# A four-layer graph network: where x is loaded and split, and where layer 2 makes its first adjacency tiles

## The chip, the cores and the metric

The kernel runs on one core of one Trainium2 chip. The metric is device time in microseconds (us) from launch to end; less is better. Three runs of the kernel before gave 3312.99, 3316.28 and 3319.8 us, median 3316.28 us.

The engines are named as in the profile: PE (TensorE, matrix products), DVE (VectorE), ACT (ScalarE), POOL (GpSimd), SP (SyncE, which here only issues transfers). Each engine works through its own list of instructions in order. A transfer is issued from the list of SP, ACT or POOL, and so it waits behind whatever stands ahead of it there.

## The reference, cut to what matters

There are 4096 nodes with 256 features, and one 0/1 adjacency matrix of 4096 x 4096. Four layers follow each other, each `x = layernorm(x + layer(x, adj))`:

```python
# layer 0
deg = jnp.sum(adj, axis=1, keepdims=True)
agg = adj @ x / jnp.maximum(deg, 1.0)
relu(jnp.concatenate([x, agg], axis=-1) @ W + b)
# layer 1: two steps of  R @ Xf  and of a top-p attention  A @ Xa, with two weights each
# layer 2
neighbor_node_features = adj @ node_features
neighbor_edge_features = jnp.einsum('ij,ji->i', adj, edge_features)[:, None]
jnp.concatenate((node_features, neighbor_node_features, neighbor_edge_features), axis=1) @ weight + bias
# layer 3: relu(D^-1/2 (adj + I) D^-1/2 x W + b)
```

## The kernel before, in words

The rows are taken in 32 tiles of 128. A product of the adjacency with a feature matrix is, for one row tile, 32 matmuls of 128x128 by 128x512 that add up in one PSUM bank. The 512 columns are the 256 features twice: the upper bits of each number and the rest. `split` (L142) makes these two halves with three instructions. DVE masks the upper bits into a buffer `up` (L145), ACT copies them into the left half (L146), and DVE subtracts them from the source into the right half (L147).

`load_halves` (L149) does this for a whole feature matrix, in eight pieces of four row tiles, here called piece 0 to piece 7. A piece is 512 KB. It is loaded into one of two buffers of `scratch`, `up` has two more, and so the load of piece c+2 waits for the subtraction of piece c. The helper is called for x in layer 0 (L222, loads issued by ACT), for features inside layer 1, and for the product z of layer 2 (L1076, loads issued by SP).

Layer 0 has two buffers for its accumulators, named acc and nef, and the row tiles take them in turns. POOL loads the adjacency as half a row tile into `a8` (L250: from float32 in DRAM to bytes, five buffers), SP stores these bytes into `adj8_d` for the later layers (L251), and ACT converts a quarter of a row tile at a time from bytes into `a` (L253, four buffers, so one row tile). A buffer of `a` becomes free when PE has multiplied with it and DVE has added it into `sums` (L260, L262; L265 folds the sums). From the sums, PE makes the degrees (L272), DVE the reciprocal (L275 to L279), ACT and DVE the scaled neighbours `agg` (L284, L285); PE transposes `x0i` and `agg` (L180) and multiplies them with w0 (L294). Row tile 2 needs the accumulator of row tile 0, so it waits for the `agg` of row tile 0. In the lists of the engines, the row tiles overlap: the order comes from a scheduler that works on the program as it is written, and it can be read from the compiled program.

At the start `list_d`, two small tables in DRAM for layer 1, is filled from the tile `blank` (L124, on SP).

Layer 2 (L1075 on) reads z from `zu_d`, into which layer 1 writes its last rows by an indirect transfer of POOL (L763). `main` (L1087) loads a quarter row tile of bytes (L1091), converts it on ACT (L1093) and multiplies (L1096). `l2_end` (L1099) loads `x2i` and `u` (L1104, L1106), and DVE adds them (L1107, L1108). All these loads are on SP.

Of the kernel before, what the change touches and what calls it, by code (L numbers as in the profile page):

```python
# [11 lines left out]
F32 = mybir.dt.float32  # L12
I32 = mybir.dt.int32
U8 = mybir.dt.uint8
F32R = mybir.dt.float32r
# [6 lines left out]
P = 128  # L22
D = 256
# [25 lines left out]
def gnn_stack(ctx, tc, x, adjt, adjn, w0, b0, w1, w2t, w3t, u1t, u2t, ln_g, ln_b, w2, b2, w3, b3, out):  # L49
# [3 lines left out]
    nc = tc.nc  # L53
    N = x.shape[0]
    NT = N // P
    LC = min(512, N)
    NLC = N // LC
    JP = min(8, NT)
    NJP = NT // JP
    J0 = min(4, NT)  # L60
# [21 lines left out]
    def load_bcast(pool, src, name):  # L82
        t = pool.tile([P, src.shape[0]], F32, name=name)
        nc.scalar.dma_start(t, src[None, :].to_broadcast([P, src.shape[0]]))
        return t
# [26 lines left out]
    list_d = [dram.tile([N + P, 1], I32, name=f"list{n}_d") for n in range(STEPS)]  # L112

    adj8_d = [dram.tile([P, NT, P], U8, name=f"adj8_{it}_d") for it in range(NT)]
# [4 lines left out]
    blank = const.tile([P, NT], I32, name="blank")  # L119
    nc.gpsimd.iota(blank, pattern=[[1, NT]], base=0, channel_multiplier=NT)  # L120
    nc.vector.tensor_scalar(blank, blank, P - 1, None, op0=ALU.bitwise_and)
    nc.vector.tensor_scalar(blank, blank, float(N), None, op0=ALU.add)
    for t in list_d:
        nc.sync.dma_start(t[:N, :].rearrange("(p k) o -> p (k o)", k=NT), blank)  # L124

    def rows(t, it):
        return t[it * P : (it + 1) * P, :]

    def all_rows(t):
        return t.rearrange("(t p) d -> p t d", p=P)  # L130

    def load_w(pool, src, name):
        t = pool.tile([P, src.shape[0] // P, src.shape[1]], F32, name=name)
        nc.scalar.dma_start(t, src.rearrange("(c p) o -> p c o", p=P))
        return t
# [3 lines left out]
        nc.gpsimd.dma_start(t, src[it, :, c * jp : (c + 1) * jp, :])  # L139
        return t  # L140

    def split(up, dst, src):  # L142


        nc.vector.tensor_scalar(up, src.bitcast(I32), UPPER, None, op0=ALU.bitwise_and)  # L145
        nc.scalar.copy(dst[:, :, :D], up.bitcast(F32))  # L146
        nc.vector.tensor_sub(dst[:, :, D:], src, up.bitcast(F32))  # L147

    def load_halves(scratch, src, queue, cols=slice(None)):  # L149


        xh = hpool.tile([P, NT, 2 * D], F32R, tag="H", name="xh")
        W = J0 * D
        for c in range(NT // J0):
            s = slice(c * J0, (c + 1) * J0)
            t, up = (scratch[:, k * W : (k + 1) * W].rearrange("p (j d) -> p j d", d=D) for k in (c % 2, 2 + c % 2))
            if queue is None:
                t = src[:, s, :]
            else:
                queue.dma_start(t, all_rows(src)[:, s, cols])  # L160
            split(up.bitcast(I32), xh[:, s, :], t)
        return xh

    def adj_matmul(pool, acc, it, halves, piece, each=None):

        for c in range(NJP):
            a = piece(it, c)
            for j in range(JP):
                jt = c * JP + j
                nc.tensor.matmul(acc, a[:, j, :], halves(jt), start=(jt == 0), stop=(jt == NT - 1))  # L170
            if each is not None:
                each(c, a)
# [24 lines left out]
    def ln_apply(dst, t, stats):  # L197
        mv, r = stats
        nc.vector.tensor_scalar(dst, t, mv[:, 0:1], r, op0=ALU.subtract, op1=ALU.mult)
# [17 lines left out]
    with tc.tile_pool(name="l0", bufs=1) as l0, tc.tile_pool(name="l0w", bufs=2) as l0w:  # L217
# [1 line left out]
        nc.scalar.dma_start(w1_sb, w1)  # L219
        w2t_sb = l0.tile([DA, DA], F32, name="w2t_sb")  # L220
        nc.scalar.dma_start(w2t_sb, w2t)
        x0h = load_halves(l0.tile([P, 4 * J0 * D], F32, name="scratch"), x, nc.scalar)  # L222
        w0_sb = load_w(l0, w0, "w0_sb")
        lb_sb = load_bcast(l0, ln_b, "lb_sb")
        b0_sb = load_bcast(l0, b0, "b0_sb")
# [5 lines left out]
                nc.scalar.copy(wq_sb[:, c, h * DA : (h + 1) * DA], ps[:, :DA])  # L231
        for h in range(2):
            nc.scalar.dma_start(w3t_sb[:, :, h * DA : (h + 1) * DA], w3t.rearrange("(c p) o -> p c o", p=P))
        x1 = xpool.tile([P, NT, D], F32, tag="X", name="x1")
        deg1 = l0.tile([P, NT], F32, name="deg1")

# [74 lines left out]
        acc = None  # L311
        for it in range(NT + 1):
            if it >= 1:
                agg = l0_agg(acc, l0_degrees(it - 1, sums))
            if it < NT:
                acc, sums = l0_main(it)
# [9 lines left out]
    with tc.tile_pool(name="l1", bufs=1, reuse_waits="tile") as l1:  # L326
# [716 lines left out]
        for n in range(STEPS):  # L1043
            cur["n"] = n
            with tc.tile_pool(name=f"step{n}", bufs=2, reuse_waits="tile") as cur["w"], \
# [6 lines left out]
                else:  # L1052
# [3 lines left out]
                    for c in range(NLC):  # L1056
                        s = slice(c * GP, (c + 1) * GP)
# [4 lines left out]
                        k = kS[:, c * LC : (c + 1) * LC].rearrange("p (j d) -> p j d", d=P)  # L1062
# [3 lines left out]
                    for c in range(NJP):  # L1066
                        s = slice(c * JP, (c + 1) * JP)
# [5 lines left out]


    with tc.tile_pool(name="l23", bufs=1, reuse_waits="tile") as l23:  # L1075
        zh = load_halves(l23.tile([P, 4 * J0 * D], F32, name="scratch"), zu_d[:N, :], nc.sync, slice(0, D))  # L1076
        w2e_sb = load_bcast(l23, w2[2 * D, :], "w2e_sb")
        b2_sb = load_bcast(l23, b2, "b2_sb")
        w3_sb = load_w(l23, w3, "w3_sb")
        b3_sb = load_bcast(l23, b3, "b3_sb")  # L1080

        yh = [pool.tile([P, NT // 2, 2 * D], F32R, tag="X", name=f"yh{k}") for k, pool in enumerate((xpool, l23))]

        def y_halves(jt):
            return yh[2 * jt // NT][:, jt % (NT // 2), :]

        def main(it, halves):  # L1087
            acc = ps_acc.tile([P, 512], F32, tag=("acc", "nef")[it % 2], name="acc")
            for c in range(NJP):
                a8 = l23.tile([P, JP, P], U8, tag="a8", name="a8", bufs=5)  # L1090
                nc.sync.dma_start(a8, adj8_d[it][:, c * JP : (c + 1) * JP, :])  # L1091
                a = l23.tile([P, JP, P], F32R, tag="adjt", name="a", bufs=4)
                nc.scalar.copy(a, a8)  # L1093
                for j in range(JP):
                    jt = c * JP + j
                    nc.tensor.matmul(acc, a[:, j, :], halves(jt), start=(jt == 0), stop=(jt == NT - 1))  # L1096
            return acc

        def l2_end(it, acc):  # L1099
            nn = l23.tile([P, D], F32, tag="agg", name="agg", bufs=2)  # L1100
            nc.scalar.copy(nn, acc[:, :D])
            nc.vector.tensor_add(nn, nn, acc[:, D:])
            xi = l23.tile([P, D], F32, tag="res", name="x2i", bufs=2)
            nc.sync.dma_start(xi, rows(x2_d, it))  # L1104
            u = l23.tile([P, D], F32, tag="u", name="u", bufs=2)
            nc.sync.dma_start(u, rows(zu_d, it)[:, D:])  # L1106
            nc.vector.tensor_add(xi, xi, b2_sb)  # L1107
            nc.vector.tensor_add(u, u, xi)  # L1108
            t = l23.tile([P, D], F32, tag="t", name="t", bufs=2)
            nc.vector.scalar_tensor_tensor(t, w2e_sb, nef[:, it : it + 1], nn, op0=ALU.mult, op1=ALU.add)  # L1110
            nc.vector.tensor_add(t, t, u)
            x3 = l23.tile([P, D], F32, tag="h", name="x3", bufs=3)
            ln_apply(x3, t, ln_stats(t))
            nc.sync.dma_start(rows(x3_d, it), x3)
            return x3

        def l2_y(it, x3):
            xt = transposed(x3)
            ps = half("mm")
            for c in range(2):  # L1120
                nc.tensor.matmul(ps, xt[:, c, :], w3_sb[:, c, :], start=(c == 0), stop=(c == 1))  # L1121
            y = l23.tile([P, 1, D], F32, tag="y", name="y", bufs=2)
            nc.scalar.activation(y[:, 0, :], ps, AF.Copy, scale=dinv[:, it : it + 1])
            up = l23.tile([P, 1, D], I32, tag="up", name="up", bufs=2)
            split(up, y_halves(it)[:, None, :], y)

        def l3_end(it, acc):
            x3 = l23.tile([P, D], F32, tag="res", name="x3i", bufs=2)
            nc.sync.dma_start(x3, rows(x3_d, it))
            a = l23.tile([P, D], F32, tag="agg", name="agg", bufs=2)  # L1130
            d = dinv[:, it : it + 1]
            nc.scalar.activation(a, acc[:, :D], AF.Copy, scale=d)
            own = y_halves(it).bitcast(F32)
            for part in (own[:, :D], own[:, D:], acc[:, D:]):
                nc.vector.scalar_tensor_tensor(a, part, d, a, op0=ALU.mult, op1=ALU.add)  # L1135
            nc.vector.tensor_add(a, a, b3_sb)
            nc.vector.scalar_tensor_tensor(a, a, 0.0, x3, op0=ALU.max, op1=ALU.add)
            o = l23.tile([P, D], F32, tag="h", name="o", bufs=3)
            ln_apply(o, a, ln_stats(a))
            nc.sync.dma_start(rows(out, it), o)  # L1140

        done = []
        for it in range(NT):
            acc = main(it, lambda jt: zh[:, jt, :])
            if it > 1:
                l2_y(it - 2, done.pop(0))
            if it > 0:
                done.append(l2_end(it - 1, last))
            last = acc
        l2_y(NT - 2, done.pop(0))  # L1150
        l2_y(NT - 1, l2_end(NT - 1, last))
        for it in range(NT):
            acc = main(it, y_halves)
            if it > 0:
                l3_end(it - 1, last)
            last = acc
        l3_end(NT - 1, last)
# [41 lines left out]
```

## Time and profile before

| what | value |
|---|---|
| median of three runs | 3316.28 us |
| the profiled execution | 3319.24 us, of which 3317.5 us are the span from first to last instruction |
| busy PE / DVE / ACT / POOL, share of the span | 91% / 72% / 57% / 24% |
| mean granted TensorE clock | 0.967 |
| first matmul of layer 0 (L170) | 43.02 us after the start of the span |
| first matmul of layer 2 (L1096) | 2790.36 us after the start of the span |

The profile is of one execution, times within it are from the start of its span. An engine that is busy is not for that reason the one that sets the time: what matters is, stage by stage, which wait ends last.

### The profile page before, as it was taken

The page shows a single profiled execution, that of the slowest core. Times are in us where ns is not written, and L with a number is a line of the kernel's source. Part 1 is how long each engine was busy: PE and PEld are TensorE (multiplying, and loading weights), DVE is VectorE, ACT ScalarE, POOL GpSimd, SP SyncE. Part 2 cuts the span into 40 slices and gives each one's busy share as a digit, 9 for nine tenths or more (in the row PEclk, how much of TensorE's full clock was granted, in tenths as well). Part 3 has the DMA queues.
Part 4 walks back from the last instruction along what each step waited for, and adds up shares of the span by engine and source line. Part 5 has one row for each costly group of instructions (what it writes and reads, how often), then busy time and mean ns, then how long its engine had stood idle before and what let it go on. Part 6 is the DMA issues. An engine that isn't in the chain of part 4 may idle for free. (4 is left out here: it accounts for less than half of the span.)

```text
span 3317.5 us, 46380 instructions
## 1 busy us (share of the span) xinstructions
PE 3005.6 (91%) x14600; PEld 2455.0 (74%) x14600; DVE 2392.3 (72%) x7113; ACT 1883.1 (57%) x3170; POOL 782.1 (24%) x916
## 2 busy tenths in 40 slices
PE   4999878999999997789989898989999786999998
PEld 4888767888888885567877777777788544888886
DVE  5888858878777776357988897888799673444444
ACT  4555566777777774455545454555455333666664
POOL 1111146666666665100000001000100001000000
PEclk9999989999999998889999999999999898999999
DMA  8888367777777776241000211011011133333332
GB/s 161 140 140 139 72 104 126 139 138 139 138 132 140 138 135 140 63 131 32 24 23 25 33 36 32 25 32 39 25 37 30 42 131 125 110 108 107 102 108 81
DMA packets 247906, 300.30 MB, mean 91 GB/s; under 512 B 34688, under 2 KB 201536, under 8 KB 247648
## 3 DMA queue, kind: packets, MB, share of 16 engines
q0 software_dynamic: 46624, 105.07, 22.7%
q1 hardware_dynamic: 184576, 176.73, 18.6%
q10 hardware_dynamic: 16448, 15.42, 1.5%
q8 instruction: 118, 1.93, 0.3%
q14 instruction: 140, 1.15, 0.1%
HBM read 331.17 MB, written 66.58 MB: 120 GB/s over the span
## 5 line engine op out<-in xcount | busy, mean ns | idle before, releaser
L657 PE MATMUL acc_r<-xh,adjq 128*128 128x512 f32 x2048 | 615.1, 431 | 25.3 <-ACT adjq L654 13.4
L742 PE MATMUL acc_bank<-xa,at 128*128 128x256 f32 x2304 | 569.6, 388 | 33.0 <-ACT at L720 32.5
L643 POOL DMA_INDIRECT G<-x_d,cols x512 | 499.4, 975 | 300.7 <-PE acc_bank L734 161.9
L742 PEld LDWEIGHTS acc_bank<-xa,at 128*128 128x128 f32 x2304 | 425.2, 194 | 94.8 <-ACT at L720 43.3
L654 ACT CAST adjq<-adj 128x512 fp32r<-128x512 uint8 x512 | 316.0, 619 | 294.5 <-PE acc_r L657 94.5
L657 PEld LDWEIGHTS acc_r<-xh,adjq 128*128 128x128 f32 x2048 | 380.4, 192 | 120.0 <-ACT adjq L654 43.5
L404 DVE MAX8 cand<-e 128x8 f32<-128x256 f32 x1024 | 381.9, 416 | 93.0 <-ACT e L386 92.0
L194 POOL TENSOR_TENSOR rstd<-ve,mhalf 128x1 f32<-128x1 f32 x168 | 102.3, 609 | 1374.4 <-DVE ve L192 1336.7
L386 ACT COPY e<-lg 128x512 f32<-128x512 f32 x552 | 319.0, 584 | 177.4 <-PE lg L385 176.4
L385 PE MATMUL lg<-kS,q 128*128 128x512 f32 x1104 | 393.5, 442 | 9.9 <-ACT e L386 9.6
L1093 ACT CAST a<-a 128x1024 fp32r<-128x1024 uint8 x256 | 268.0, 1048 | 147.5 <-PE acc L1096 119.3
L734 PE MATMUL acc_bank<-G,dg 128*128 128x256 f32 x1024 | 276.6, 390 | 51.5 <-DMA G<-x_d,cols 40.4
L501 DVE FIND_INDEX8 cols<-top,e 128x8 uint32<-128x4096 f32 x64 | 282.8, 4419 | 0.0
L1096 PE MATMUL acc<-xh,a 128*128 128x512 f32 x1024 | 254.9, 402 | 16.9 <-ACT a L1093 13.2
L170 PE MATMUL acc<-xh,a 128*128 128x512 f32 x1024 | 257.9, 404 | 13.3 <-ACT a L253 13.3
L734 PEld LDWEIGHTS acc_bank<-G,dg 128*128 128x128 f32 x1024 | 194.0, 193 | 101.1 <-DMA G<-x_d,cols 48.9
L720 ACT COPY at<-at_ps 128x512 f32<-128x512 f32 x296 | 173.6, 588 | 114.0 <-PE at_ps L717 90.1
L1096 PEld LDWEIGHTS acc<-xh,a 128*128 128x128 f32 x1024 | 190.5, 189 | 60.3 <-ACT a L1093 15.2
L1096 PE MATMUL acc<-yh,a 128*128 128x512 f32 x1024 | 233.7, 390 | 0.0
L170 PEld LDWEIGHTS acc<-xh,a 128*128 128x128 f32 x1024 | 191.7, 190 | 55.1 <-ACT a L253 13.5
L1096 PEld LDWEIGHTS acc<-yh,a 128*128 128x128 f32 x1024 | 192.1, 188 | 39.8
L253 ACT CAST a<-a 128x1024 fp32r<-128x1024 uint8 x128 | 133.9, 1048 | 129.6 <-PE acc L170 117.4
(282 smaller groups left out, 5001.5 us busy)
## 6 DMA issues: line engine op xcount, KB each, us to landing
adj<-adj_d SPq DMA_DIRECT2D x256, 128.0 KB, 2.7
a<-adj_d SPq DMA_DIRECT2D x256, 128.0 KB, 2.3
a<-in_adjt POOLq DMA_DIRECT2D x64, 256.0 KB
adj_d<-a SPq DMA_DIRECT2D x64, 256.0 KB, 3.7
adjn<-in_adjn POOLq DMA_DIRECT2D x64, 256.0 KB
x_d<-x SPq DMA_DIRECT2D x65, 128.0 KB, 1.8
G<-x_d,cols POOLq DMA_INDIRECT x512
xf_d<-xf_new SPq DMA_DIRECT2D x64, 128.0 KB, 4.9
```

Of the source, the lines that this page charges most:

```text
L170: nc.tensor.matmul(acc, a[:, j, :], halves(jt), start=(jt == 0), stop=(jt == NT - 1))
L385: nc.tensor.matmul(pl[:, :LC], q[k], kS[:, s], start=(k == 0), stop=(k == 1))
L386: nc.scalar.copy(l[:, s], pl[:, :LC])
L404: nc.vector.max(dst[:, 8 * g : 8 * g + 8], src[:, g * GW : (g + 1) * GW])
L501: nc.vector.max_index(st["at"][:, 8 * r : 8 * r + 8], t8, st["e"][:, :N])
L643: nc.gpsimd.indirect_dma_start(out=g, out_offset=None, in_=x1_d, in_offset=bass.IndirectOffsetOnAxis(ap=st["at"][:, k : k + 1], axis=0))
L654: nc.scalar.copy(a, cur["a8"][:, g % 2 * GP : (g % 2 + 1) * GP, :])
L657: nc.tensor.matmul(acc_r, a[:, j, :], xf[:, jt, :], start=(jt == 0), stop=False)
L734: nc.tensor.matmul(acc_a, dg[:, k % 4, :], st["G"][k], start=(k == 0), stop=(k == KEPT - 1))
L742: nc.tensor.matmul(acc_a, ats[g][:, j, :], cur["xa"][:, jt, :], start=(jt == 0), stop=(jt == NT - 1))
L1093: nc.scalar.copy(a, a8)
L1096: nc.tensor.matmul(acc, a[:, j, :], halves(jt), start=(jt == 0), stop=(jt == NT - 1))
```

## The change

In layer 0, x's pieces are loaded by SP instead of ACT, with four buffers for the loaded pieces instead of two (`up` keeps two), and the copy of the upper half is made by DVE instead of ACT. The fill of `list_d` is written after the loads of x. In layer 2, the first row tile's four adjacency loads and conversions are written ahead of the loads and splits of z; `main` uses `adj_matmul`, the helper that layer 0 uses, with the same matmuls in the same order as written. The helpers used by layers 1 and 2 keep two buffers and ACT's copy.

```diff
-    for t in list_d:
-        nc.sync.dma_start(t[:N, :].rearrange("(p k) o -> p (k o)", k=NT), blank)
...
-    def split(up, dst, src):
+    def split(up, dst, src, copy=nc.scalar.copy):
...
-        nc.scalar.copy(dst[:, :, :D], up.bitcast(F32))
+        copy(dst[:, :, :D], up.bitcast(F32))
...
-    def load_halves(scratch, src, queue, cols=slice(None)):
+    def load_halves(scratch, src, queue, cols=slice(None), ahead=2, copy=nc.scalar.copy):
...
-            t, up = (scratch[...] for k in (c % 2, 2 + c % 2))
+            t, up = (scratch[...] for k in (c % ahead, ahead + c % 2))
...
-        x0h = load_halves(l0.tile([P, 4 * J0 * D], F32, name="scratch"), x, nc.scalar)
+        x0h = load_halves(l0.tile([P, 6 * J0 * D], F32, name="scratch"), x, nc.sync, ahead=4, copy=nc.vector.tensor_copy)
...
+        for t in list_d:
+            nc.sync.dma_start(t[:N, :].rearrange("(p k) o -> p (k o)", k=NT), blank)
...
     with tc.tile_pool(name="l23", bufs=1, reuse_waits="tile") as l23:
+        def piece(it, c):
+            a8 = l23.tile([P, JP, P], U8, tag="a8", name="a8", bufs=5)
+            nc.sync.dma_start(a8, adj8_d[it][:, c * JP : (c + 1) * JP, :])
+            a = l23.tile([P, JP, P], F32R, tag="adjt", name="a", bufs=4)
+            nc.scalar.copy(a, a8)
+            return a
+
+        ahead = [piece(0, c) for c in range(NJP)]
         zh = load_halves(l23.tile([P, 4 * J0 * D], F32, name="scratch"), zu_d[:N, :], nc.sync, slice(0, D))
...
-            for c in range(NJP):
-                a8 = l23.tile([P, JP, P], U8, tag="a8", name="a8", bufs=5)
-                nc.sync.dma_start(a8, adj8_d[it][:, c * JP : (c + 1) * JP, :])
-                a = l23.tile([P, JP, P], F32R, tag="adjt", name="a", bufs=4)
-                nc.scalar.copy(a, a8)
-                for j in range(JP):
-                    jt = c * JP + j
-                    nc.tensor.matmul(acc, a[:, j, :], halves(jt), start=(jt == 0), stop=(jt == NT - 1))
+            adj_matmul(l23, acc, it, halves, lambda it, c: ahead.pop(0) if ahead else piece(it, c))
```

More of the change, by code (lines that the diff above doesn't have):

```diff
@@ L155, in load_halves @@
             s = slice(c * J0, (c + 1) * J0)
-            t, up = (scratch[:, k * W : (k + 1) * W].rearrange("p (j d) -> p j d", d=D) for k in (c % 2, 2 + c % 2))
+            t, up = (scratch[:, k * W : (k + 1) * W].rearrange("p (j d) -> p j d", d=D) for k in (c % ahead, ahead + c % 2))
             if queue is None:
@@ L160, in load_halves @@
                 queue.dma_start(t, all_rows(src)[:, s, cols])
-            split(up.bitcast(I32), xh[:, s, :], t)
+            split(up.bitcast(I32), xh[:, s, :], t, copy)
         return xh
```

## The prediction

> **What bounds the kernel now.** I read the windows by stage first: from 60 us to the end of layer 0 PE is busy in all of every window, so whatever lets PE start earlier is handed on to the end. Two stretches are not like that, the first 60 us and 2778 to 2820, and both hold the change. In the timeline of the start (start, duration, engine, operation, in brackets the idle time and its releaser):
>
> ```profile
> 16.03 0.69 DVE L145 TENSOR_SCALAR scratch<-scratch 128x1024 int32<-128x1024 int32 x1 [14.95 <-DMA scratch<-in_x]
> ...
> 20.36 0.69 DVE L145 TENSOR_SCALAR scratch<-scratch 128x1024 int32<-128x1024 int32 x1 [2.37 <-DMA scratch<-in_x]
> 21.08 1.04 ACT L146 CAST xh<-scratch 128x1024 fp32r<-128x1024 f32 x1 [3.28 <-DVE scratch L145]
> 21.08 1.23 DVE L147 TENSOR_TENSOR xh<-scratch 128x1024 fp32r<-128x1024 f32 x1
> 21.09 1.63 ACTq L160 DMA_DIRECT2D scratch<-in_x  x2
> ...
> 41.93 1.04 ACT L253 CAST a<-a 128x1024 fp32r<-128x1024 uint8 x1
> 43.02 2.50 PE L170 MATMUL acc<-xh,a 128*128 128x512 f32 x5 [13.26 <-ACT a L253]
> ...
> 43.77 1.23 DVE L147 TENSOR_TENSOR xh<-scratch 128x1024 fp32r<-128x1024 f32 x1
> ```
>
> Piece 0 needs until 16.03, piece 1 until 20.36. Pieces 2 and 3 are issued only at 21.09, behind ACT's copies, and each next pair again, so piece 7 is split at 45.00 (43.77 + 1.23). PE starts at 43.02, after ACT's first conversion, which stands behind seven copies. Why 16 us for 512 KB: the DMA view from 8 to 12 us (packets, MB, share of 16 engines):
>
> ```profile
> q0 software_dynamic: 192, 0.36, 88.8%
> q10 hardware_dynamic: 192, 0.20, 17.4%
> ```
>
> POOL's five adjacency loads (q0) and ACT's queue (q10) alternate packet by packet, and a q0 packet costs an engine 0.296 us (0.888 x 4 us x 16 / 192) against 0.058. At layer 2, the chain that ended last reads (start, duration, what):
>
> ```profile
> 2778.54 4.99 DMA zu_d<-e,to_l
> 2783.55 3.44 DMA scratch<-zu_d
> 2787.01 0.70 DVE scratch L145
> 2787.74 1.22 DVE xh L147
> 2788.97 0.62 DVE scratch L145
> 2789.61 1.24 DVE xh L147
> 2790.86 4.98 DMA scratch<-zu_d
> ```
>
> It is z's loads, two at a time, not ACT's conversions.
>
> **What the skill says.** "DMA: Bandwidth & Descriptors", Queues, rings and completion order: an engine goes round the queues that have work; 192 to 192 above agrees. The same page, Issuing engines are not separate DMA queues: another issuing engine saves only issue time. So SP's queue is no extra bandwidth. "VectorE: DVE Perf Modes", The perf-mode tier table: float32 copies within SBUF, like tensor_scalar, run at 2x, tensor_tensor at 1x; the trace agrees for the latter two (0.69 and 1.23 us for 1024).
>
> **The change at the start, step by step.**
> 1. Requests. Pieces 0 to 3 stand first on SP. ACT's first issue is at 0.81 and its bytes flow at 2.1; q0's flow at 3.2. About 1.1 us ahead of q0 at 390 GB/s, shared with w1, gives x some 20 of its 32 packets per engine and piece (512 packets of 1 KB over 16). q0 has 45 per engine (5 loads x 144 / 16). Against q0 and ACT's w0, lb and b0, a round of three costs 0.296 + 2 x 0.058 = 0.41. Piece 1 is complete 44 rounds later: 3.2 + 18.1 = 21.3, with 0.7 for completion (estimate: piece 6's bytes stop at 39.6, its mask starts 40.25) **22.0**; 20.36 before. So more loads in flight bring piece 1 no earlier; pieces 2 and 3 follow at about 23.5 and 25, instead of 25.14 and about 28.
> 2. DVE's copy is not in the trace before at this size. From below 0.55 (its rate in the 2x form), from above 1.23 (the 1x subtraction); I take the 0.69 of the mask. A piece then costs 0.69 + 0.69 + 1.23 + 0.04 = 2.65 where it was 1.95. Seven from 22.0, and `blank`'s two (0.35): 40.9. DVE becomes the bound of this stage.
> 3. Collision. ACT's conversions no longer stand behind copies; two at about 23 free the first a8, and its refill on POOL also waits for the store on SP, behind piece 5 and the two list transfers (0.42 each, nothing waits for them until layer 1). It starts about 33 and meets piece 7 (issued after piece 3's subtraction, about 31): 9 packets x 0.296 = 2.7 us later at most; slack in DVE's list about 2. I take 0.8: **piece 7 split at 41.7**.
> 4. PE multiplies row tile 0 along with the splits, but the gain isn't all kept. In the compiled order the sums follow the last split on DVE: 14 adds for row tiles 0 and 1 (14 x 0.69 = 9.7), folds (2 x 0.71), degrees, first sums of row tile 2 (2 x 0.69), agg (0.48): 13.7 us to agg of row tile 0, which row tile 2 needs. It starts at 41.7 + 14.1 = 55.8 (60.43 before). Row tile 3: 32 matmuls (7.4), w0 product (1.5), transposes and degrees (0.5) later, 65.2, against 70.28 (DVE ends the sums of row tile 2 about 20 us after the last split: it has caught up). **Gain 5.1.** Bounds: piece 1 at 19.3 instead of 22 (a bigger head start) gives 7, limited by pieces 2 and 3; the copy at 1.23 takes 3.8 off; a full collision 1.9.
> 5. Free: removed ACT copies (8 x 1.04) only release conversions, which then wait for a; x0i's transposes come before the first matmul, while PE waits anyway (0.4 gained).
>
> **At layer 2.** The four conversions (4.2 us) move to before z, into ACT's idle time until 2787; their loads precede z's on SP, which waits 44.5 us there. PE may start about 2789. But at 2808.52 it has used every piece it had and waits for pieces 6 and 7:
>
> ```profile
> 2808.52 11.55 PE L1096 MATMUL acc<-xh,a 128*128 128x512 f32 x48 [2.13 <-ACT xh L146]
> ```
>
> So only piece 7, split at 2810.30, counts. Its chain keeps two buffers. Odd pieces landed 5.1, 3.8 and 4.4 us after issue; the first was beside five other loads that now come before or after, and may save 0.8. Two of l2_end's adds (0.43) fall between odd pieces' steps. On SP, piece 7 now stands behind a row tile 3 load that waits for an ACT conversion (about 2802.7; piece 7's own wait ends about 2803.5). **Gain 0.5**, from -1 to +1.2.
>
> **Sum.** 5.1 + 0.5 = 5.6. The profiled execution of 3319.24 would be 3313.6; it is 3.0 above the median of 3316.28, inside the runs' spread, so I set 3310.7.
>
> **The rivals.**
> - *Pieces come earlier than I reckon.* If SP's head start is longer, DVE is the only bound; with piece 0 split before 10 us and pieces 2 and 3 at 22, piece 7 is split at about 39 and with layer 2 the gain is 8 to 9.5. For it: ACT's first bytes come 1.3 us after issue, POOL's later. Against: q0's 45 packets still take 13.3 us of every engine. About 3307.5.
> - *A wait takes the place of the old one.* DVE's longer split (2.65 against 1.95) and the collision in full, copy at 1.23: piece 7 at about 46, sums after it; gain 5.1 - 3.8 - 1.1 = 0.2. About 3316.
> - *Slower: refills crowd x out.* Early conversions let POOL refill three a8 buffers instead of one before piece 7 lands: 27 packets x 0.296 = 8 us beside pieces 5 to 7, with the copy at 1.23 another 3.8: piece 7 at about 52.7, a loss of 6 to 7. It decides from piece 7 later than 46.8 (no gain) and 53 (over 0.2%). Against it: stores ahead of refills are in SP's list behind pieces 5 to 7. About 3323.
> - *No change* because the start is hidden: excluded by PE's full windows up to 360 us.
>
> **Chances.** A measurement of this kernel can tell about 0.2%, 6.6 us, from no change. My forecast (gain 2 to 8.5) has 0.66, of which 0.31 lies over 6.6, since the head start is steep: every 5 packets are 2 us. Earlier pieces 0.14, all faster. New wait 0.10, within. Crowding, and reuse of moved memory in layers 1 and 2 that I can't price, 0.10, slower. Faster 0.45, within 0.45, slower 0.10. Range 3305 to 3318: the early case to the new wait, with the runs' spread.
>
> **What would show it.** Piece 0's mask before 10 us, piece 1's at 20 to 23; from piece 1 to piece 7 DVE without gaps; DVE's copy 0.6 to 0.7; the last subtraction ending 40 to 43.5; row tile 2's first matmul at 54 to 57; in layer 2 the first matmul near 2789 less the shift, but the unbroken run of matmuls 0 to 1.5 us earlier in its stage. It is wrong if piece 1 lands before 17, if the last split is after 47, or if row tile 2 follows it by under 12 us.

## The result and the profile after

| | median of the runs | ratio to before, 95% interval | profiled execution (span) |
|---|---|---|---|
| before | 3319.65 us (20 runs) | | 3319.24 us (3317.5 us) |
| after | 3307.27 us (20 runs) | 0.9967 (0.9959 to 0.9974) | 3313.77 us (3312.0 us) |

The change makes the kernel faster by 0.33%, about 11 us (0.0033 x 3319.65). The forecast was 3310.7 us with a range of 3305 to 3318, so the time lies inside it, 3.4 us below the point. The gain does not fit so well: 5.6 us were forecast, about half of what came. The two profiled executions stand only 5.5 us apart. They are single executions, and the runs of after lie between 3299 and 3318 us, so the stages below are compared by the times of their events and not by the two totals. Line numbers of after: the mask is L142, the copy L143, the subtraction L144, x's loads L157, the matmul with the adjacency L167, layer 0's conversions L252, its sums L259 and L261, the degrees L271, agg L284, the w0 product L293.

The timeline of DVE at the start of after (start, duration, engine, line, operation, in brackets the idle time before it and its releaser):

```profile
5.20 0.69 DVE L142 TENSOR_SCALAR scratch<-scratch 128x1024 int32<-128x1024 int32 x1 [4.17 <-DMA scratch<-in_x]
5.93 0.69 DVE L143 CAST xh<-scratch 128x1024 fp32r<-128x1024 f32 x1
...
7.67 0.69 DVE L142 TENSOR_SCALAR scratch<-scratch 128x1024 int32<-128x1024 int32 x1
...
17.95 0.69 DVE L142 TENSOR_SCALAR scratch<-scratch 128x1024 int32<-128x1024 int32 x1 [7.64 <-DMA scratch<-in_x]
...
24.62 0.69 DVE L142 TENSOR_SCALAR scratch<-scratch 128x1024 int32<-128x1024 int32 x1 [5.89 <-DMA scratch<-in_x]
...
25.83 1.22 DVE L144 TENSOR_TENSOR xh<-scratch 128x1024 fp32r<-128x1024 f32 x1
...
34.82 0.69 DVE L142 TENSOR_SCALAR scratch<-scratch 128x1024 int32<-128x1024 int32 x1 [0.75 <-DMA scratch<-in_x]
...
37.77 1.22 DVE L144 TENSOR_TENSOR xh<-scratch 128x1024 fp32r<-128x1024 f32 x1
38.91 0.69 DVE L259 TENSOR_TENSOR sums<-a 128x512 f32<-128x512 f32 x1
```

Pieces 0 and 1 are both there by 7.67, where piece 1 used to come at 20.36. Then DVE waits 7.64 us for piece 2 and 5.89 us for piece 3. Piece 2's copy and subtraction (25.83) stand behind piece 3's mask in DVE's list, so they wait for piece 3 as well. From piece 3 on DVE is nearly without gaps, and the last subtraction ends at 38.99 (37.77 + 1.22) instead of 45.00. The DMA view says why, first from 4 to 8 us and then from 8 to 12 us (queue, packets, MB, share of 16 engines; q1 is SP's queue, q0 POOL's, q10 ACT's):

```profile
q1 hardware_dynamic: 807, 0.79, 63.0%
q0 software_dynamic: 75, 0.15, 37.8%
q10 hardware_dynamic: 188, 0.11, 8.9%
...
q0 software_dynamic: 173, 0.32, 79.9%
q1 hardware_dynamic: 173, 0.18, 15.5%
q10 hardware_dynamic: 173, 0.18, 12.8%
```

POOL issues its loads at 1.59 us as before, but its packets flow only from about 6.2 us (before: 3.2). By then SP's queue has moved some 70 packets per engine, among them all 64 of pieces 0 and 1. From then on the three queues take turns, 173 to 173 to 173, and pieces 2 and 3 come at the pace of q0's packets.

PE in the same stretch, and its windows (length, then busy time and instructions of each engine, then PEclk, DMA share, GB/s):

```profile
27.98 7.33 PE L167 MATMUL acc<-xh,a 128*128 128x512 f32 x24
37.40 1.44 PE L167 MATMUL acc<-xh,a 128*128 128x512 f32 x4 [2.08 <-DVE xh L144]
...
51.46 0.45 PE L177 MATMUL tr<-ident,agg 128*128 128x128 f32 x2 [1.41 <-DVE agg L284]
51.66 1.96 PE L167 MATMUL acc<-xh,a 128*128 128x512 f32 x4
53.41 2.77 PE L293 MATMUL mm_bank<-w_sb,xt 128*128 128x256 f32 x8
55.83 6.86 PE L167 MATMUL acc<-xh,a 128*128 128x512 f32 x28
...
62.88 1.88 PE L167 MATMUL acc<-xh,a 128*128 128x512 f32 x7
```

```profile
38.00:41.00 3.00, 2.79 (x8) 1.51 (x7) 2.86 (x4) 1.05 (x1) 0.00 (x0) 0.52 1.05 143
42.00:49.00 7.00, 7.00 (x32) 5.49 (x30) 6.62 (x15) 5.12 (x6) 1.59 (x3) 1.00 0.79 102
...
52.00:55.00 3.00, 3.00 (x8) 2.35 (x8) 2.50 (x5) 0.53 (x1) 0.00 (x0) 0.50 1.03 158
```

PE starts 15 us earlier (27.98 against 43.02), waits 2.08 us for piece 6, and waits again between 49 and 51.5 for row tile 0's agg. Soon after each wait its granted clock is 0.5 for 3.4 us (38.1 to 41.5 and 51.8 to 55.2). Row tile 2 starts at 51.66 (60.43 before), row tile 3 at 62.88 (70.28 before). The last degrees of layer 0 (L271) stand at 367.58 instead of 374.59. So in this pair of traces the start gives 7.0 to 7.4 us.

Layer 2 in the timeline of after:

```profile
2774.83 3.88 ACT L1079 CAST a<-a 128x1024 fp32r<-128x1024 uint8 x4 [1.31 <-issue]
2778.96 0.92 SPq L157 DMA_DIRECT2D scratch<-zu_d  x2
...
2784.57 3.91 PE L167 MATMUL acc<-xh,a 128*128 128x512 f32 x8 [11.68 <-DVE xh L144]
...
2803.76 11.55 PE L167 MATMUL acc<-xh,a 128*128 128x512 f32 x48 [2.12 <-ACT xh L143]
```

The conversions are early. The first matmul comes 5.61 us after z's first loads are issued, where it was 6.81 (2790.36 - 2783.55). But the unbroken run of 48 starts 24.80 us after that issue, where it was 24.97 (2808.52 - 2783.55).

### The profile page after: what moved, and what is told of

It is laid out like the page before. It is cut to its first block, busy times and chain, and to the rows that moved or that the text cites. A ratio compares the mean times of both kernels' runs of the same rounds, so it can differ in the third digit from the quotient of the medians.

```text
span 3312.0 us, 46373 instructions
## 1 busy us (share of the span) xinstructions
PE 3017.6 (91%) x14600; PEld 2465.7 (74%) x14600; DVE 2393.5 (72%) x7121; ACT 1873.9 (57%) x3162; POOL 782.7 (24%) x916
## 3 DMA queue, kind: packets, MB, share of 16 engines
q14 instruction: 140, 1.15, 0.1%
## 5 line engine op out<-in xcount | busy, mean ns | idle before, releaser
L167 PE MATMUL acc<-xh,a 128*128 128x512 f32 x2048 | 516.5, 405 | 17.8 <-DVE xh L144 14.0
L167 PEld LDWEIGHTS acc<-xh,a 128*128 128x128 f32 x2048 | 384.6, 191 | 103.0 <-ACT xh L143 17.0
L733 PE MATMUL acc_bank<-G,dg 128*128 128x256 f32 x1024 | 277.8, 392 | 51.5 <-DMA G<-x_d,cols 40.6
L167 PE MATMUL acc<-yh,a 128*128 128x512 f32 x1024 | 233.7, 390 | 0.0
L252 ACT CAST a<-a 128x1024 fp32r<-128x1024 uint8 x128 | 133.5, 1048 | 157.4 <-PE acc L167 121.3
L167 PEld LDWEIGHTS acc<-yh,a 128*128 128x128 f32 x1024 | 192.2, 188 | 39.6
L384 PEld LDWEIGHTS lg<-kS,q 128*128 128x128 f32 x1104 | 182.9, 192 | 32.5 <-ACT e L385 19.4
L716 PE MATMUL at_ps<-ident,e 128*128 128x128 f32 x1184 | 183.5, 279 | 22.0 <-issue 13.8
```

The source lines that it names most:

```text
L384: nc.tensor.matmul(pl[:, :LC], q[k], kS[:, s], start=(k == 0), stop=(k == 1))
L716: nc.tensor.transpose(ps[:, j, :], e[:, (g * G + j) * P : (g * G + j + 1) * P], ident)
L733: nc.tensor.matmul(acc_a, dg[:, k % 4, :], st["G"][k], start=(k == 0), stop=(k == KEPT - 1))
```

## The experiments

Each kernel is compared with runs of the kernel before on its own chip. On one of the chips the kernel before took 3309 us, on another 3350 to 3352, so only ratios and times within the first 400 us are set side by side. "Row tile 3" is its first matmul, "end" the last degrees of layer 0; times in us.

| kernel | last split ends | first matmul | row tile 2 | row tile 3 | end | ratio to before (95%) |
|---|---|---|---|---|---|---|
| before | 45.00 | 43.02 | 60.43 | 70.28 | 374.59 | |
| after | 38.99 | 27.98 | 51.66 | 62.88 | 367.58 | 0.9967 (0.9959 to 0.9974) |
| c_after, the same on another chip | 38.94 | 27.59 | 51.52 | 62.59 | 367.25 | 0.9966 (0.9954 to 0.9978) |
| e1 start only | 38.85 | 27.97 | 51.51 | 62.63 | 366.74 | 0.9965 (0.9951 to 0.9978) |
| e2 layer 2 only | 46.18 | 44.56 | 61.92 | 71.77 | 376.07 | 0.9997 (0.9990 to 1.0004) |
| e3 copy on ACT | 34.48 | 28.53 | 46.96 | 56.66 | 360.87 | 0.9945 (0.9932 to 0.9959) |
| e3_again | 34.73 | 28.61 | 46.36 | 56.06 | 360.75 | 0.9956 (0.9937 to 0.9976) |
| e4 two buffers | 49.82 | 26.04 | 55.81 | 65.66 | 370.23 | 0.9979 (0.9971 to 0.9986) |
| e5 ACT's queue | 38.79 | 33.97 | 51.90 | 61.73 | 366.33 | 0.9965 (0.9951 to 0.9980) |
| e6 POOL held | 39.73 | 23.09 | 52.37 | 63.58 | 369.29 | 0.9967 (0.9954 to 0.9980) |
| e7 no head start | 42.39 | 27.72 | 55.37 | 64.97 | 369.59 | 0.9965 (0.9953 to 0.9977) |
| e8 x first | 33.37 | 25.58 | 45.63 | 55.24 | 359.81 | 0.9954 (0.9937 to 0.9970) |
| e10 filled PE | 39.42 | 27.46 | 51.41 | 61.03 | 365.75 | 0.9963 (0.9951 to 0.9976) |
| e11 four buffers only | 40.96 | 43.10 | 61.65 | 71.51 | 376.19 | 0.9991 (0.9978 to 1.0005) |

The intervals are 5 to 13 us wide, so the ratios tell e4 and e11 from the whole change, and hardly the others. The times at the start are far sharper: two traces each of after and of e3, on different chips, agree within 0.6 us on row tile 3. The kernel before and e2, whose starts are the same, differ by 1.5.

**Which half carries it: e1 and e2.** e1 takes layer 2's loop from the kernel before, e2 takes everything else from it.

```diff
 e1, in layer 2:
-        ahead = [piece(0, c) for c in range(NJP)]
 e2, in layer 0:
-        x0h = load_halves(l0.tile([P, 6 * J0 * D], ...), x, nc.sync, ahead=4, copy=nc.vector.tensor_copy)
+        x0h = load_halves(l0.tile([P, 4 * J0 * D], ...), x, nc.scalar)
```

> x by SP, four pieces in flight, DVE copies; layer 2 as before. Theory (the start carries the gain): first matmul of row tile 2 at 51.7 us and row tile 3 at 62.9 as with the whole change, all of layers 0 and 1 earlier by 7 us; time 7 to 11 us below the kernel before (ratio 0.9967 to 0.9979), within 1 us of the whole change. Rival (layer 2's conversions carry a part): still 7 us earlier up to the end of layer 1, but the time only 5 to 7 us below before, and 3 to 4 us above the whole change.

> The start as before; layer 2's first four conversions ahead of z's splits. Theory: the first matmul of layer 2 comes about 1.2 us earlier after z's last transfer into DRAM has landed, but the unbroken run of 48 matmuls, which waits for z's piece 7, starts 24.8 us after that landing instead of 25.0: time within 1 us of before (ratio 0.9997 to 1.0000). Rival (the conversions were in the way and carry 3 to 4 us): the run of 48 starts about 21.5 us after the landing, ratio 0.9988 to 0.9990.

e1 has the whole gain, e2 none that can be told. From z's first issue to the long run of matmuls it is 24.92 us in e1 (2761.02 to 2785.94), with layer 2 as before, and 24.76 in e2 (2771.74 to 2796.50), with the conversions ahead. Together with 24.97 before and 24.80 after, layer 2's part is 0.2 us. e1's ratio of 0.9965 lies just beyond the far end of its first theory (0.9967), and the rival is out. Side by side on this one chip, e1 has row tile 3 9.1 us earlier than e2, and the end 9.3 us earlier.

**Which edit of the start: e3, e4, e5 and e11.** One part each is undone (e3, e4, e5), or one part alone is put into the kernel before (e11). The later place of `list_d`'s fill was not undone by itself.

```diff
-        x0h = load_halves(l0.tile([P, 6 * J0 * D], ...), x, nc.sync, ahead=4, copy=nc.vector.tensor_copy)
 e3, copy on ACT:
+        x0h = load_halves(l0.tile([P, 6 * J0 * D], ...), x, nc.sync, ahead=4)
 e4, two buffers:
+        x0h = load_halves(l0.tile([P, 4 * J0 * D], ...), x, nc.sync, copy=nc.vector.tensor_copy)
 e5, ACT's queue:
+        x0h = load_halves(l0.tile([P, 6 * J0 * D], ...), x, nc.scalar, ahead=4, copy=nc.vector.tensor_copy)
 e11, in the kernel before:
-        x0h = load_halves(l0.tile([P, 4 * J0 * D], ...), x, nc.scalar)
+        x0h = load_halves(l0.tile([P, 6 * J0 * D], ...), x, nc.scalar, ahead=4)
```

> The whole change, but the copy of x's upper halves stays on ACT. Theory (the bytes of pieces 2 to 7 set the splits, and after the last split the sums do): DVE has 8 x 0.69 us less to do, but pieces land as late; piece 7 split at 37.5 to 39 against 38.99, and ACT's first conversions stand behind copies (last of row tile 0 near 42), so row tile 2 starts at 50.5 to 53 against 51.66: time within 2 us of the whole change. Rival 1 (DVE's longer split is the bound): piece 7 split at 35 or earlier, row tile 2 near 48, 3 to 4 us better than the whole change. Rival 2 (freeing ACT was what brought the gain): row tile 2 at 56 or later, 4 us or more worse.

> The whole change, but with two buffers for x's pieces instead of four. Theory (the gain at the start comes from pieces 0 and 1 passing ahead of POOL's queue, not from the four buffers): pieces 0 and 1 masked at 5.2 and 7.7 as with four; pieces 2 and 3 issued after the splits of 0 and 1 at 8 and 10.5, so they share every round with POOL's packets and are masked near 20 and 25 (17.95 and 24.62 with four); piece 7 split at 39 to 41.5, row tile 2 at 52 to 54.5: 0.5 to 3 us of the gain lost. Rival (four in flight is what brings it): piece 7 split after 43, row tile 2 after 56, 5 us or more of the gain lost.

> The whole change, but x's loads issued by ACT as before, with four in flight. ACT issues them from 2.0 us, SP from 0.8, POOL from 1.6. Theory (SP's queue only buys that pieces 0 and 1 pass ahead of POOL's packets; DVE's splits then set the end): piece 0 masked near 16 and piece 1 near 20.4 as in the kernel before, but pieces 2 and 3 at 22 to 24; DVE then has seven splits of 2.65 in a row, last split 39 to 40.5, first matmul near 30, row tile 3 at 62 to 64.5 (62.88 with the whole change): 0 to 2 us of the gain lost. Rival (the pass ahead of POOL carries the gain): last split after 42, row tile 3 after 66, 4 us or more of it lost.

> The kernel before with four buffers for x's loaded pieces instead of two, and nothing else: ACT issues the loads and copies. Theory (what the change buys at the start is loads that do not wait for copies two pieces back; queue and copying engine are worth little): piece 0 masked near 16, piece 1 near 20.4, the later ones every 2 to 2.5 us, last split 34 to 38 (45.0 before), the first matmul behind ACT's copies at 34 to 38, no gap in PE, row tile 3 at 59 to 63: 7 to 11 us below before, as much as the whole change. Rival (the queue or DVE's copy is needed): last split after 41, row tile 3 after 66, less than 4 us of gain.

e3 falls to its rival 1: DVE's longer split was a bound. DVE and PE in its timeline:

```profile
18.17 0.69 DVE L142 TENSOR_SCALAR scratch<-scratch 128x1024 int32<-128x1024 int32 x1 [9.02 <-DMA scratch<-in_x]
...
18.90 1.23 DVE L144 TENSOR_TENSOR xh<-scratch 128x1024 fp32r<-128x1024 f32 x1
...
32.13 2.35 DVE L144 TENSOR_TENSOR xh<-scratch 128x1024 fp32r<-128x1024 f32 x2
34.40 0.68 DVE L259 TENSOR_TENSOR sums<-a 128x512 f32<-128x512 f32 x1
...
28.53 16.15 PE L167 MATMUL acc<-xh,a 128*128 128x512 f32 x58
...
46.96 1.18 PE L167 MATMUL acc<-xh,a 128*128 128x512 f32 x4
47.98 1.99 PE L293 MATMUL mm_bank<-w_sb,xt 128*128 128x256 f32 x8
...
56.66 1.87 PE L167 MATMUL acc<-xh,a 128*128 128x512 f32 x7
```

The last split ends 4.5 us earlier, row tile 2 follows 12.5 us after it as in after (11.6 in e3_again), and PE runs 58 matmuls without a wait. Then the w0 product takes 1.99 instead of 2.77, and row tile 3 starts 6.2 us earlier than in after. So moving the copy to DVE, taken by itself beside the other edits, costs 6 us at the start. In the totals, e3's median is 5.3 us below that of e1, which ran on the same chip (3291.11 and 3296.38).

Not all of this is the time of the copies, because the compiled order changes with the edit. In e3, piece 2's subtraction follows its own mask (18.90), while in after it waits for piece 3 (25.83). SP's list changes too: the loads of pieces 6 and 7 stand ahead of the stores of the adjacency in e3 and behind the first of them in after. An estimate from the two timelines: from piece 3's mask on, after has six copies more, 0.60 us each from start to start, and one subtraction more, 1.14. That is 4.7 us, and 4.5 were seen. Piece 2's share of it, 1.7 us, is a matter of order and could have been done while DVE waited. No run tried that order with the copy on DVE.

e4 falls to its rival: with two buffers the last split ends at 49.82, later than in the kernel before, and row tile 3 is 2.8 us later than in after. That is less than expected of the rival, since nine of the fourteen sums of row tiles 0 and 1 now sit in DVE's gaps between the splits, and row tile 2 follows the last split by 6.0 us instead of 12.7. In the totals it is the rival's size: e4's median is 5.4 us above that of e1, on the same chip.

e5 keeps everything although its piece 0 is masked only at 16.15:

```profile
33.97 13.78 PE L167 MATMUL acc<-xh,a 128*128 128x512 f32 x50 [1.36 <-ACT a L252]
...
51.90 1.64 PE L167 MATMUL acc<-xh,a 128*128 128x512 f32 x6
53.38 1.89 PE L293 MATMUL mm_bank<-w_sb,xt 128*128 128x256 f32 x8
...
61.73 1.66 PE L167 MATMUL acc<-xh,a 128*128 128x512 f32 x6
```

Its last split ends with that of after (38.79 and 38.99), PE begins 6 us later (4 later than expected), and yet row tile 3 is 1.15 us earlier (0.86 against c_after, on the same chip): its clock is 1.00 in all windows from 34 to 66 us. So the head start of pieces 0 and 1 is worth nothing here, and neither is SP's queue as long as DVE copies. The Trainium skill ("DMA: Bandwidth & Descriptors", Issuing engines are not separate DMA queues) agrees: another issuing engine saves issue time, not transfer time.

e11 was expected to bring the whole gain and brings none at the start (end 376.19). The loads do come earlier, the last split by 4.0 us. But ACT's list is the same chain:

```profile
39.73 1.04 ACT L146 CAST xh<-scratch 128x1024 fp32r<-128x1024 f32 x1 [1.87 <-DVE scratch L145]
...
41.99 3.89 ACT L253 CAST a<-a 128x1024 fp32r<-128x1024 uint8 x4
```

The first conversion stands behind all eight copies (41.99, before 41.93, after 23.84), and PE starts at 43.10. Set side by side, with four buffers each, row tile 3 is at

| | loads by ACT | loads by SP |
|---|---|---|
| copy by ACT | 71.51 (e11) | 56.06 and 56.66 (e3) |
| copy by DVE | 61.73 (e5) | 62.59 to 62.88 (after) |

Loads and copies both on ACT keep its conversions until the last piece. Taking either away frees them. Taking the loads away is the cheaper way, since DVE, whose splits and sums are the next bound, then stays as it was. Taking both away, as the change does, pays for one of them without need. (e11 has the fill of `list_d` and layer 2 as in the kernel before. e2 shows that layer 2 doesn't matter here; the fill is untested.)

One rule fits most of these kernels: row tile 2 starts at the later of first matmul + 17.4 (PE has two row tiles to do) and last split + 12.6 (DVE has their sums to do). Before: 60.4 and 57.6, PE's start decides. After: 45.4 and 51.6, the sums decide. e3: 45.9 and 47.1. e5: 51.4 and 51.4. e11 starts 1.1 later than its 60.5, because its first 14 matmuls have the slow pace of PE's beginning and in before only the first 8 do. The rule misses e3_again by 1.0 (46.4, and the rule says 47.3) and e10 by 0.6, and it doesn't hold for e4, whose sums are not all behind the splits. It was drawn from the traces afterwards and fitted to them.

**The head start and POOL: e6, e7, e8.**

```diff
 e6: +                if c == 3: nc.gpsimd.tensor_copy(gate, t[:, 0, :1])           # after the load of piece 3
     +                    if it == 0 and c == 0: nc.gpsimd.tensor_copy(a8[:, 0, :4].bitcast(F32), gate)
 e7: +                if c < ahead: nc.vector.tensor_copy(t[:DA, 0, :1], w1_sb[:, :1])  # before the load
 e8: +            nc.sync.dma_start(x1[:, c * J0 : (c + 1) * J0, :], all_rows(x)[:, c * J0 : (c + 1) * J0, :])
     +        x0h = load_halves(l0.tile([P, 4 * J0 * D], ...), x1, None)             # split out of x1, copy on ACT
     +                    if it == 0 and c == 0: nc.gpsimd.tensor_copy(a8[:, 0, :4].bitcast(F32), x1[:, 3 * J0, :1])
```

> The whole change, and POOL's first adjacency loads wait (through a one-column copy on POOL) until x's piece 3 has landed. Theory (POOL's packets hold up pieces 2 and 3 and leave DVE idle 7.6 and 5.9 us): pieces 2 and 3 masked by 11 to 14 us, DVE splits without a gap up to piece 5, last split 29 to 34, row tile 2 at 42 to 47, row tile 3 at 52 to 57 (62.88): 6 to 11 us below the whole change, ratio to before 0.9935 to 0.995. Rival (the adjacency, 8 us later, takes the place of x): the first conversions come after 24 us, row tile 2 at 50 or later, within 2 us of the whole change or slower.

> The whole change, but x's first four loads wait until w1 has landed (a one-column copy on DVE), so that their bytes come after POOL's have begun. Theory (without the pass ahead every piece shares its rounds with POOL's packets): piece 0 masked at 15 to 18, piece 1 at 21.5 to 24, then seven splits in a row, last split 40.5 to 43.5, 1.5 to 4.5 later than with the whole change; the first matmul later too, with fewer gaps in PE after it; row tile 3 at 63.5 to 66.5; 1 to 4 us of the gain lost. Rival (the pass ahead does not matter, since DVE or the sums set the end): last split within 1 us of 38.99, time within 1 us of the whole change.

> Three edits on top of the whole change: x's eight pieces are loaded by SP straight into the tile of layer 0's result (all eight in flight), the copy of the upper halves is back on ACT, and POOL's first adjacency loads wait for x's piece 3. Theory (the bound was the wait for pieces and DVE's 2.65 us a piece): all pieces landed by 13 to 18 us, last split 20 to 24, then DVE's sums, row tile 2 at 33 to 38, row tile 3 at 43 to 48, and no gap in PE after its first matmul: 15 to 20 us below the whole change, ratio to before 0.9895 to 0.993. Rival (the adjacency now comes late): row tile 0's conversions wait for POOL's loads until after 24 us, row tile 3 at 54 or later, no better than the version with ACT's copy alone (0.9945).

e7 ends where its theory says: last split at 42.39, row tile 3 at 64.97, 2.1 to 2.4 us later than in after. The way there is another. Piece 0 is masked at 21.14 instead of 15 to 18, five us later than in e5, and the first matmul is no later than in after. So e7 takes away more than the head start, and in the total (0.9965) no loss can be told.

e5 and e7 fit a sum that the prediction had: from the mask of piece 1 to the last split DVE needs 18.3 us in e5 (20.46 to 38.79) and 18.65 in e7 (23.74 to 42.39). Without a head start the last split follows piece 1. With it, in after, the last split follows piece 3, masked at 24.62. So the head start pays only if piece 1 would otherwise come later than about 20.6 us (an estimate, 38.99 less 18.4). This was read from the traces afterwards.

e6's theory fell. SP and DVE in its timeline:

```profile
19.46 0.33 SPq L255 DMA_DIRECT2D adj_d<-a  x1
19.88 0.99 SPq L157 DMA_DIRECT2D scratch<-in_x  x2
...
31.66 0.69 DVE L142 TENSOR_SCALAR scratch<-scratch 128x1024 int32<-128x1024 int32 x1 [10.22 <-DMA scratch<-in_x]
...
35.56 0.69 DVE L142 TENSOR_SCALAR scratch<-scratch 128x1024 int32<-128x1024 int32 x1 [3.20 <-DMA scratch<-in_x]
```

Pieces 2 and 3 come early as expected (masked at 10.45 and 12.51). But in SP's list a store of the adjacency stands ahead of pieces 6 and 7. It waits for POOL's first load, which now comes late, and the two pieces are issued at 19.88, in the middle of POOL's packets: DVE waits 10.22 us for piece 6. The wait was moved from piece 2 to piece 6, not removed. e8 has its loads ahead of the stores and still sees it, with pieces 6 and 7 masked at 20.02 and 30.41. It starts row tile 3 at 55.24, 0.8 to 1.4 us ahead of e3, and not at 43 to 48. The transfers of x and POOL's five loads want the same engines, and either order leaves a hole in the splits.

**The halved clock: e10 and c_after.**

```diff
+                if (it, c) in ((0, 2), (1, NJP - 1)):
+                    spare = ps_lg.tile([P, 512], F32, tag="lg", name="spare")
+                    n = (14, 9)[it]
+                    for k in range(n):
+                        nc.tensor.matmul(spare, a[:, k % JP, :], x0h[:, k, :], start=(k == 0), stop=(k == n - 1))
```

> The whole change plus 23 extra matmuls of 128x128 by 128x512 into a spare PSUM bank that nobody reads: 14 in row tile 0, where PE waits for x's piece 6, and 9 after row tile 1, where PE waits for row tile 0's agg. Theory (after a wait of about 2 us in PE its granted clock is halved for some 3.5 us, and the second of these stretches lies on row tile 2's path): no stretch at 0.5 between 38 and 56 us, row tile 2 at 51.3 to 52, its w0 product 1.9 instead of 2.77, row tile 3 at 60.6 to 61.5 instead of 62.88; more work and 1.4 to 2.3 us less time. Rival (the clock falls with the work, not with the waits): the stretches at 0.5 stay or grow, row tile 3 at 62.9 or later.

> The changed kernel itself, so that it stands on the same chip as the others: ratio 0.996 to 0.9975; row tile 3 at 62 to 63.5 with the two stretches of halved clock.

> The whole change with the copy left on ACT, on the same chip as the changed kernel. Theory (6 us less at the start, of which 4.5 are DVE's eight copies and 1.7 the halved clock): row tile 3 at 56 to 57.5, 5 to 8 us below the changed kernel, ratio to before 0.994 to 0.9955. Rival (its advantage was that chip's): within 2 us of the changed kernel.

PE and two of its windows in e10:

```profile
48.96 2.25 PE L260 MATMUL spare<-xh,a 128*128 128x512 f32 x9
...
51.41 1.86 PE L167 MATMUL acc<-xh,a 128*128 128x512 f32 x7
53.11 1.89 PE L298 MATMUL mm_bank<-w_sb,xt 128*128 128x256 f32 x8
...
61.03 1.89 PE L167 MATMUL acc<-xh,a 128*128 128x512 f32 x7
```

```profile
38.00:41.00 3.00, 2.19 (x8) 1.14 (x7) 2.86 (x5) 0.90 (x1) 0.00 (x0) 1.00 1.04 132
52.00:55.00 3.00, 3.00 (x15) 2.58 (x14) 2.86 (x7) 1.22 (x3) 0.53 (x1) 1.00 1.00 206
```

With 23 matmuls more to do, no window falls to 0.5, PE does 15 matmuls between 52 and 55 us where it did 8, and row tile 3 starts 1.56 us earlier than in c_after on the same chip. The four traces with a wait of about 2.4 us ahead of row tile 2 (after, c_after, e1, e6) all have a stretch at 0.5 right behind it. So the effect is shown at the start. In the total it can't be told (0.9963 and 0.9966). c_after came as expected. e3_again repeats e3's start within 0.6 us, 6.5 ahead of c_after; its median is 3336.11 against 3339.32, inside both intervals, so on that chip the expected 5 to 8 us are not confirmed by the totals.

**What stays open.** The ratios say 11 us, and at the end of layer 0 the traces show 7.0 (after against before, 367.58 and 374.59) to 9.3 (e1 against e2, on one chip). Layer 2 adds 0.2. The remaining 1.5 to 4 us are not placed. For e1 and e2 the profiled executions are also the medians: they are 11.0 us apart, 9.3 at the end of layer 0 and 1.7 after it. On the other chip such a difference can't be read from single traces: from the end of layer 0 to the end of the span its eight profiled kernels (e5 to c_after and e3_again), alike there but for layer 2's order in e11, take 2955.6 (e7) to 2986.9 us (e3_again). A gain of 9.5 us (9.3 and 0.2) lies inside the intervals of after, c_after and e1, so there need be no rest. No experiment looked for one.

## Why the prediction was right, and which steps were off

The time lies inside the range of 3305 to 3318. The gain, 11 us, is twice the 5.6 that were set and lies above the 2 to 8.5 given for this forecast, and above the 8 to 9.5 of its rival of earlier pieces. That the time is inside owes something to luck. The forecast started from 3316.28, the median of three runs, and the kernel before has 3319.65 in twenty. From 3316.28 the ratio gives 3305.3, just inside the lower end.

The direction and the place held: the gain that the traces place is made in the first 60 us but for 0.2, PE hands it on, and z's piece 7 decides in layer 2. The mechanism held in its second half, from DVE's splits to the sums to row tile 2, and failed in its first, the arrival of the pieces. Of what it said would show it, these came: piece 0 before 10 us, the copy of 0.69, layer 2's first matmul (2789 less the shift of 4.6 makes 2784.4, and 2784.57 was seen) and its long run 0.17 us earlier. Piece 1, DVE without gaps, the last split at 40 to 43.5 and row tile 2 at 54 to 57 did not.

Row tile 3 gained 7.40 us between the traces of before and after (9.1 between e2 and e1), and the prediction had 5.1. Its steps, in order:

1. **Requests: mis-sized.** The step took some 20 of piece 0's 32 packets per engine ahead of POOL's queue, and so piece 1 at 22.0. The trace has all of pieces 0 and 1 ahead, 64 packets, and piece 1 by 7.67. The prediction had named piece 1 before 17 us as a sign of being wrong, and this step is wrong. The round of three queues that it went on to use is right (173 each), and the Trainium skill ("DMA: Bandwidth & Descriptors", Queues, rings and completion order) agrees that the queues take turns. The term that failed is the moment at which POOL's queue begins. x's bytes flow from about 2 us, as the step took, but it left POOL's at the 3.2 us of the kernel before, and they came at 6.2. The trace before had a hint of it: there POOL's loads were issued first, and x, issued by ACT at 2.04, flowed only from about 6.1. What it cost: the rival of earlier pieces had the right arrival for pieces 0 and 1 and the right last split, about 39, but pieces 2 and 3 came at 17.95 and 24.62, not at 22. For the total, e5 shows that the head start hardly matters, because its piece 1 is there at 20.46 and its pieces 2 and 3 at 23 without it.
2. **DVE's copy: right in size, and DVE the bound from piece 3 on.** 0.69 as taken. e3 adds what the step did not say: it was avoidable, 4.5 us at the last split with the order that goes with it. The step took the splits one after another as well, and the compiled order put piece 2's subtraction behind piece 3's mask.
3. **Collision: smaller than taken.** Piece 7 waited 0.75 us in DVE's list, but the last split was at 38.99 instead of 41.7, since pieces 0 and 1 were out of DVE's way long before.
4. **Sums: the right bound, 1.4 us too long.** 12.67 from last split to row tile 2 instead of 14.1. e3, e6 and c_after repeat it with 12.5 to 12.6, e3_again has 11.6.
5. **Row tile 3 (still step 4 of the prediction): a term was missing.** Row tile 3 was put 9.4 us behind row tile 2; it is 11.22 in after, 9.62 to 9.70 in e10 and e3. The term is the halved clock. The forecast gave PE an earlier start with waits in it and did not price what a wait does to the matmuls after it. The Trainium skill says it ("TensorE: Matmul & The Clock Gate", The HAM clock gate): an idle window of about 3.4 us halves the clock, and it takes a busy window to get it back. The trace agrees on one half and on 3.4 us, but not on how long PE has to be idle (2.08 us in after).

Together: 5.1 + 2.7 (points 1 and 3) + 1.4 (point 4) - 1.8 (point 5) = 7.4. Three errors of 1.4 to 2.7 us partly cancel, which is luck too, and leave 2.3. They account for the start; the rest of the way to 11 us is not placed, as said above. Layer 2's 0.5 was 0.2, in its bounds. The claim that ACT's freed copies cost and bring nothing beyond earlier conversions missed their weight: e11 against e3 and e5 shows that the conversions' place in ACT's list is the greater part of the gain.

Of the rivals, the earlier pieces came nearest in time (3307.5) and in the last split, with only a part of its mechanism. The new wait in place of the old did not come in after, but it did in e6. Crowding by refills was not seen.

## What to carry to other kernels

When one engine issues loads, copies and converts, first take away the job that costs other engines least. Here that was issuing, and moving the copy too cost 6 us, since it made DVE the next bound. After such an edit, read the compiled lists again: which step of one piece now stands behind another piece? A transfer that is put ahead of another does not make the two shorter: look which piece waits instead. And an earlier start of PE is worth its full time only if work follows without long waits. At this start, waits of about 2 us were followed by 3.4 us in which a matmul took 628 ns instead of 397, and spare matmuls in the waits took that away.

## What the runs showed of the hardware that was not expected

- Waits of 2.08 us (after) and of about 2.4 us with a few small matmuls in between were followed by 3.4 us at clock 0.5. Waits of 0.9 us (e8) were not. In e7, waits of 1.69 and 0.63 us close to each other were followed by 6.8 us at 0.5. All these stretches are near a multiple of 3.4 us (13.7 in e4). But the length of a wait does not decide alone: the 2.12 us that PE waits in layer 2 were followed by 3.4 us at 0.5 in c_after, where the run of 48 matmuls takes 12.82 us, and by none in before, after, e1 and e2 (11.55 us in before and after). What else decides was not tried. The Trainium skill ("TensorE: Matmul & The Clock Gate", The HAM clock gate) speaks of an idle window of about 3.4 us; here less sufficed.
- The record of the clock has no entry before its first change (31.3 us in after, 46.6 in before), and the windows print 1.00 there. The pace shows otherwise: in after the first five matmuls take 629 ns in the median, as in the stretch at 0.5 (628), and 397 from 32 to 35 us. How long the slow pace lasts differs from run to run: 8 matmuls in the kernel before, 14 in e11.
- The queue that comes second starts late. POOL's loads, issued at the same 1.59 us, have their first packets at about 3.2 us where ACT's x loads follow them and at 6.2 us where SP's x loads precede them; in e8, issued at 13.22 beside loads in flight, after 17.5. SP's and ACT's queues do the same behind POOL's: x flows from about 6.1 us in the kernel before (issued by ACT at 2.04) and from about 7.5 in e7 (issued by SP at 3.16). That is 4.1 to 4.6 us after the issue, against 1.2 to 1.6 for the first in line. Why queues that take turns start so late was not tried.
